# Another order of positions in theta/phi's first product, and a ScalarE copy moved ahead of the last plain half

## The chip, the cores and the metric

One core of one Trainium2 chip runs the whole program. The metric is the device time of one execution in microseconds, the median over several runs.

## The reference

Two layers work on eight images of 512 channels by 1024 positions (32 by 32), all in fp32. Cut to what matters:

```python
# layer 0: attention over positions, 8 heads of 64 channels
q, k, v = (conv1x1(x, W, b) for W, b in ((Wq, bq), (Wk, bk), (Wv, bv)))   # 512 -> 512
attn = softmax(einsum('bhdn,bhdm->bhnm', q, k) / 8)
x = x + conv1x1(einsum('bhnm,bhdm->bhdn', attn, v), Wp, bp)
# layer 1: non-local block, 256 inner channels
g, theta, phi = (conv1x1(x, w, b) for w, b in (g, theta, phi))            # 512 -> 256
f = einsum('bcn,bdn->bcd', theta, phi) / n
z = conv1x1(einsum('bcd,bdn->bcn', f, g), W, Wb) + x
out = batchnorm(z)                     # mean and variance over all images and positions
```

## The kernel before

**Images and stages.** `unshifted` walks over the images in a loop `for b in range(B)`. For each image it runs attention, then the projections q, v and k of image b+1 (`heads_of`, `values`), then the output projection of image b (`project`, PSUM tiles `pp`), theta and phi (`theta_phi`, tiles `ptp`), g (`pg`), and the product with W (`pz`).

**Products by quarters.** A matrix product is split as Strassen's scheme with Winograd's sums does it: seven products of quarter matrices in place of eight, with sums and differences made on VectorE (DVE) and GpSimd (POOL). Some of the seven are nested, which means that the quarter product is again split into seven small ones.

- `six` makes q, v and k of images 1 to 7. Its function `plain` first makes the one product that isn't nested, in two halves of 128 output channels. Each half goes to a PSUM bank of its own and is read twice by ScalarE (ACT) through `begin`: once into a temporary, `T6` (in the profile `T_pq` or `T_pk`), and once into the quarter "11" of the result (`q` or `k`). Then `six` goes through three pairs of nested products in the hand-written order

```python
    ORDER = "0a 0b 1a 2a 2b 1b 5a 4a 5b 4b 3a 3b 6a 6b".split()
```

where the digit is the small product and the letter the member of the pair. Each small product is added into PSUM, on top of what its chain already holds, and what the chain holds is read out before the next product of that chain is put on top. Where the reading is the first one of a result quarter, it is a ScalarE copy (line 479); otherwise it is a VectorE add (line 481). In the first pair, member a goes to quarter "11" (adds) and member b to quarter "12" (copies). Small products 0, 2 and 4 of a member share one chain; 1 and 3 share another. The four PSUM tiles s0 to s3 are used in turn: the plain halves take two of them, the four slots of the first pair are taken after these, and so slot 2 (products 1a, 5a, 3a) reuses the tile of the first plain half and slot 3 (products 1b, 5b, 3b) that of the second.

- `project` ends, for images 1 to 6, with the nested product `(1, "21", "11")`: its small products are added by VectorE (line 504) onto quarter "11" of the image `x`, which is channel blocks 0 and 1 and positions 0 to 511. These adds come in pieces of one channel block and 256 positions. In the order of the small products (`SEVEN`) the last four pieces are: block 0 positions 256 to 511, block 1 positions 256 to 511, block 0 positions 0 to 255, block 1 positions 0 to 255.

- `theta_phi` calls `seven` with `inner="tp"` for images 1 to 7. Its first product, "11", multiplies quarter "11" of `x` by a weight quarter. Positions are the rows of the result, so `x` is the operand that is loaded as weights: four parts i of 128 positions, and for each part two matmuls, one for each channel block k (line 391).

**What sets the order.** The framework's planner orders the instructions of each engine by its own cost model, except where the kernel pins one behind everything traced ahead of it on its engine (`pe`, `dve`, `sp`). All matmuls are pinned, and most VectorE sums here. The ScalarE reads of the plain halves and the copies are not pinned. The engines wait for one another by semaphores, and a matmul's wait sits on its weight load.

**How a matmul shows.** Each fp32 matmul of the program appears as two records of TensorE (PE), each with a weight load (PEld) of its own.

Of the kernel before, what the change touches and what calls it, by code (L numbers as in the profile page):

```python
# [10 lines left out]
AF = mybir.ActivationFunctionType  # L11
# [5 lines left out]
P = 128  # L17
# [13 lines left out]
def unshifted(ctx: ExitStack, tc: tile.TileContext, a: dict, out: bass.AP):  # L31
    nc = tc.nc
# [320 lines left out]
    def seven(name, w, data, positions_out, first, add, between=None, early=False,  # L353
              by_chunk=False, inner=None, via=()):

        nk, half = w.shape[2], w.shape[3]
        tags = list(free)
        free[:] = [tags[3], tags[1], tags[0], tags[2]] if early else [tags[3], tags[1], tags[2], tags[0]]  # L360
        slots, begun = {}, set()
        steps, counts = iter(()), iter(())
        if inner:
            free[:] = [tags[0], tags[2], tags[1], tags[3]] if inner == "p" else [tags[1], tags[2], tags[3], tags[0]]
            products, goes_to, counts = INNER[inner]
            counts = iter(counts)
            steps = nested(name, w, data, tags[2:], first, add, goes_to, positions_out)
        else:
            products = LATER if early == "later" else EARLY if early else SEVEN

        def read(reads, ps):
            for to, is_first in reads:
                (first if is_first else add)(to, ps)

        for n, (what, wi, di, s, reads) in enumerate(products):
            if s not in slots or early and what == "t4" or inner == "p" and what == "s3t3":
                slots[s] = bank(tags[s], f"{name}_{s}_{n}")
                begun -= {one for one in begun if one[0] == s}
            ps, d = slots[s], data[di]
            if positions_out:  # L380
                parts = [(ps.rearrange("p h (i f) -> p (h i) f", f=half)[:, i, :], i * half // 512,
                          lambda k, i=i: d[:, k, i * P:(i + 1) * P], lambda k: w[:, wi, k, :])
                         for i in range(512 // P)]
            else:
                parts = [(ps[:, m, :], m, lambda k, m=m: w[:, wi, k, m * P:(m + 1) * P], lambda k: d[:, k, :])
                         for m in range(half // P)]
            work = [(*part, k) for part in parts for k in range(nk)]
            if by_chunk and what in ("11", "s1t1"):
                work.sort(key=lambda one: one[4])
            for i, (to_ps, at, lhsT, rhs, k) in enumerate(work):  # L390
                pe(nc.tensor.matmul(to_ps, lhsT(k), rhs(k), start=(s, at) not in begun, stop=(k == nk - 1),  # L391
                                    skip_group_check=True))
                begun.add((s, at))
                for _ in range(next(counts, 0)):
                    next(steps)
            if inner and what in via:
                via[what](reads, ps)
            else:
                read(reads, ps)
            if between and n in between:  # L400
                between[n]()
# [4 lines left out]
    def six(name, w, data, positions_out, at, begin, third, fills, by_scalar=False, later=None):  # L406

        fills = dict(fills)
        shape = [P, 4, 256] if positions_out else [P, 2, 512]
        temps = {}  # L410

        def to(q):
            if q[0] != "T":
                return at(q)
            if q not in temps:
                temps[q] = w3.tile(shape, F32, tag="acc", name=f"{q}_{name}")
            return temps[q]

        def piece(q, i, j):
            if positions_out:  # L420
                return to(q)[:, j * 2:j * 2 + 2, i * P:(i + 1) * P]
            return to(q)[:, i, j * 256:(j + 1) * 256]

        def add(q, of, engine=None):
            dve((engine or nc.gpsimd).tensor_tensor(to(q), to(q), to(of), ALU.add))

        def plain():
            d = data["11"]
            for half in range(2):
                ps = next_bank(f"{name}_0_{half}")[:, 0, :]  # L430
                if positions_out:
                    ps = ps.rearrange("p (i f) -> p i f", f=256)
                for i in range(2 if positions_out else 1):
                    for k in range(2):
                        if positions_out:
                            at = (half * 2 + i) * P
                            pe(nc.tensor.matmul(ps[:, i, :], d[:, k, at:at + P], w[:, 0, k, :],  # L437
                                                start=(k == 0 and i == 0), stop=(k == 1), skip_group_check=True))
                        else:
                            pe(nc.tensor.matmul(ps, w[:, 0, k, half * P:(half + 1) * P], d[:, k, :],  # L440
                                                start=(k == 0), stop=(k == 1), skip_group_check=True))
                for q in ("T6", "11"):
                    at_ = to(q)[:, half * 2:half * 2 + 2, :] if positions_out else to(q)[:, half, :]
                    begin(at_, ps, half)
            load_w("first")

        plain()
        for one in fills.pop("plain", ()):
            one()
        for n, pair in enumerate(SIX):  # L450
            if n == 2:
                add("12", "22")
                add("12", "T6")
                for one in fills.pop("middle", ()):
                    one()
            slots = [next_bank(f"{name}_in_{n}_{i}") for i in range(4)]
            free[:] = [free[2], free[3], free[0], free[1]]
            begun = set()
            for step, which in enumerate(ORDER):
                _, wi, di, chain, reads = SEVEN[int(which[0])]  # L460
                m = "ab".index(which[1])
                outer, of, q = pair[m]
                a, d = w.inner(outer)[wi], data[f"inner {of}"][di]
                ps = slots[m if not chain else 2 + m][:, chain // 2, :256]
                start = (m, chain) not in begun
                begun.add((m, chain))
                if positions_out:
                    ps = ps.rearrange("p (i f) -> p i f", f=P)
                    for i in range(2):
                        pe(nc.tensor.matmul(ps[:, i, :], d[:, i * P:(i + 1) * P], a, start=start and not i, stop=True,  # L470
                                            skip_group_check=True))
                else:
                    pe(nc.tensor.matmul(ps, a, d, start=start, stop=True, skip_group_check=True))  # L473
                for (i, j), is_first in reads:
                    i, j = int(i) - 1, int(j) - 1
                    if is_first and q == "T7":
                        third(piece(q, i, j), ps, piece("T6", i, j), i)
                    elif is_first and q not in ("11", "T6"):
                        nc.scalar.copy(piece(q, i, j), ps)  # L479
                    else:  # L480
                        dve(nc.vector.tensor_tensor(piece(q, i, j), piece(q, i, j), ps, ALU.add))  # L481
                for one in fills.pop((n, step), ()):
                    one()
            load_w()
        assert not fills, fills
        if by_scalar:
            add("T7", "T6")
        ends = [lambda q=q: add(q, "T7") for q in ("22", "21")]
        if later is not None:
            later += ends  # L490
            return
        for one in ends:
            one()
# [68 lines left out]
    def heads_of(b, what, w, bias, data, pin=lambda ins: None, steps=None, fills=None, **how):  # L562
# [2 lines left out]

        if fills is not None:
            def begin(to, ps, i):
                nc.scalar.activation(to, ps, AF.Identity, bias=bias[:, i:i + 1])

            def third(to, ps, of, i):  # L570
                if what == "q":
                    nc.scalar.activation(to, ps, AF.Identity, bias=steps[:, i:i + 1])
                else:
                    dve(nc.vector.scalar_tensor_tensor(to, ps, steps[:, i:i + 1], of, ALU.add, ALU.add))

            six(f"p{what}_{b}", w, data, False, lambda q: t[:, rows(q), cols(q)], begin, third, fills,
                what == "q", how.get("later"))
            return t
# [919 lines left out]
```

## Time and profile before

| | |
|---|---|
| median of three runs | 2102.07 us (2102.05 to 2102.19) |
| profiled execution, its own time | 2102.2 us |
| its span, first to last instruction | 2100.4 us |
| TensorE busy | 2076.9 us (99%) |
| VectorE busy | 1442.6 us (69%) |
| ScalarE busy | 803.0 us (38%) |
| GpSimd busy | 818.3 us (39%) |
| mean granted TensorE clock | 0.996 |

The span is 1.8 us shorter than the execution's own time; the rest lies ahead of the first instruction and after the last. Busy TensorE time is a sum of records that overlap (a matmul's record ends after the next one has started), so a short wait can lie inside it.

### The profile page before, as it was taken

Reading aid. Unit: us, or ns where it says so; the run is one execution under the profiler, and the core shown is the slowest. Engines: PE = TensorE matmul, PEld = TensorE weight load, DVE = VectorE, ACT = ScalarE, POOL = GpSimd, SP = SyncE. Lnnn points to the kernel's source line nnn. Section 1 sums busy time; section 2 is a strip of 40 time slices with the busy share of each in tenths; the row PEclk is TensorE's granted clock in tenths of the full one; section 3 lists DMA queues with packets and bytes.
Section 4 is the critical chain, followed back from the end, with each engine's and each line's share of the span. In section 5 each row is a group of like instructions: output and inputs, shape, how many; then the busy total and the mean of one; then the engine's idle time right before and its main releaser. Section 6 shows DMA issues by size and latency. Waiting matters only on the chain.

```text
span 2100.4 us, 34471 instructions
## 1 busy us (share of the span) xinstructions
PE 2076.9 (99%) x13682; PEld 1176.0 (56%) x13682; DVE 1442.6 (69%) x2192; ACT 803.0 (38%) x1071; POOL 818.3 (39%) x689
## 2 busy tenths in 40 slices
PE   9999999999999999999999999999999999999995
PEld 4535864358733677336773377633876348743472
DVE  5587668775678656876567765677665775676756
ACT  1465204652046420564205641066312653056106
POOL 0024900448413583134922358223681338711010
PEclk9999999999999999999999999999999999999998
DMA  6254634445343443435324363153644345322668
GB/s 230 83 145 78 184 116 153 46 89 154 106 116 39 100 141 103 119 40 116 133 90 123 40 146 121 69 126 40 157 142 164 38 47 180 99 31 39 218 253 322
DMA packets 79697, 248.71 MB, mean 118 GB/s; under 512 B 17316, under 2 KB 25768, under 8 KB 77480
## 3 DMA queue, kind: packets, MB, share of 16 engines
q1 hardware_dynamic: 65656, 220.07, 32.3%
q0 software_dynamic: 12016, 24.80, 12.2%
q8 instruction: 110, 1.80, 0.4%
q10 hardware_dynamic: 1856, 1.56, 0.3%
q14 instruction: 59, 0.48, 0.1%
HBM read 164.64 MB, written 48.17 MB: 101 GB/s over the span
## 4 chain that ended last, share of the span: by engine, by line
PE 98%; ACT 1%; DVE 1%; DMA 0%; issue 0%
PE ps L638 21%; PE po L664 21%; PE ptp L391 7%; PE pv_in L470 6%; PE pp L391 6%; PE pk_in L473 6%; PE pq_in L473 6%; PE pg L391 5%; PE pz L391 3%; PE pp_in_s L342 3%; PE pf L916 2%; PE ptp_in_s L339 2%; PE pwf L959 1%; PE pv L437 1%; PE pq L440 1%; PE pq L391 1%
## 5 line engine op out<-in xcount | busy, mean ns | idle before, releaser
L641 ACT ACTIVATE e<-ps 128x1024 f32<-128x1024 f32 x512 | 523.0, 1025 | 412.0 <-PE ps L638 400.5
L694 POOL DMA_DIRECT2D fold<-acc x336 | 257.1, 816 | 921.7 <-DMA fold<-acc 543.3
L647 DVE TENSOR_TENSOR acc<-acc,e 128x1024 f32<-128x1024 f32 x384 | 469.9, 1224 | 93.2 <-ACT e L641 82.2
L638 PE MATMUL ps<-q,k 64*64 64x512 f32 x4096 | 529.2, 589 | 0.0
L664 PE MATMUL po<-e,v 64*64 64x512 f32 x4096 | 528.7, 589 | 0.0
L664 PEld LDWEIGHTS po<-e,v 64*64 64x64 f32 x4096 | 156.6, 133 | 282.9 <-issue 275.4
L638 PEld LDWEIGHTS ps<-q,k 64*64 64x64 f32 x4096 | 155.5, 133 | 283.2 <-issue 275.3
L947 ACT ACTIVATE g<-pg,gb 128x512 f32<-128x512 f32 x31 | 21.3, 688 | 366.5 <-PE pg L391 366.4
L645 DVE TENSOR_TENSOR acc<-e,e 128x1024 f32<-128x1024 f32 x64 | 78.3, 1224 | 114.5 <-ACT e L641 112.2
L391 PE MATMUL pp<-t_o,w_WpT 128*128 128x512 f32 x208 | 102.0, 592 | 0.0
L391 PE MATMUL ptp<-w_tp,t_x 128*128 128x256 f32 x400 | 96.1, 379 | 0.0
L756 POOL TENSOR_TENSOR o<-o,r 128x1024 f32<-128x1024 f32 x28 | 65.5, 2361 | 31.8 <-DMA r<-den_d 31.5
L391 PEld LDWEIGHTS ptp<-w_tp,t_x 128*128 128x128 f32 x400 | 72.3, 190 | 7.8
L821 POOL TENSOR_TENSOR x<-x,read 128x1024 f32<-128x1024 f32 x30 | 69.8, 2353 | 13.0 <-ACT read L818 13.0
L481 DVE TENSOR_TENSOR k<-k,pk_in 128x256 f32<-128x256 f32 x112 | 46.8, 421 | 39.5 <-PE pk_in L473 35.0
L391 PE MATMUL ptp<-w_tp,x 128*128 128x256 f32 x272 | 70.0, 381 | 0.8
L479 ACT COPY v<-pv_in 128x256 f32<-128x256 f32 x84 | 31.4, 374 | 95.0 <-DVE T_pv L481 25.5
L479 ACT COPY k<-pk_in 128x256 f32<-128x256 f32 x84 | 31.3, 372 | 92.0 <-PE pk_in L473 90.3
L481 DVE TENSOR_TENSOR v<-v,pv_in 128x256 f32<-128x256 f32 x112 | 46.3, 421 | 29.3 <-PE pv_in L470 22.8
L470 PE MATMUL pv_in<-w_WvT,i_t_x 128*128 128x128 f32 x448 | 59.2, 275 | 0.0
L473 PE MATMUL pk_in<-i_t_x,w_WkT 128*128 128x256 f32 x224 | 58.1, 381 | 0.1
L473 PE MATMUL pq_in<-i_t_x,w_WqT 128*128 128x256 f32 x224 | 57.5, 379 | 0.0
(250 smaller groups left out, 3249.6 us busy)
## 6 DMA issues: line engine op xcount, KB each, us to landing
fold<-acc POOLq DMA_DIRECT2D x336, 64.0 KB, 3.0
w_WqT<-kept_WqT SPq DMA_DIRECT2D x21, 896.0 KB, 5.8
w_WvT<-kept_WvT SPq DMA_DIRECT2D x21, 896.0 KB, 5.4
w_WkT<-kept_WkT SPq DMA_DIRECT2D x21, 896.0 KB, 6.6
r<-den_d SPq DMA_DIRECT2D x32, 512.0 KB, 6.8
x<-in_x_dram SPq DMA_DIRECT2D x30, 512.0 KB, 5.8
spill<-x SPq DMA_DIRECT2D x24, 512.0 KB, 4.0
z<-spill SPq DMA_DIRECT2D x24, 512.0 KB, 8.4
```

Source lines behind the costliest of these rows:

```text
L391: pe(nc.tensor.matmul(to_ps, lhsT(k), rhs(k), start=(s, at) not in begun, stop=(k == nk - 1), skip_group_check=True))
L470: pe(nc.tensor.matmul(ps[:, i, :], d[:, i * P:(i + 1) * P], a, start=start and not i, stop=True, skip_group_check=True))
L473: pe(nc.tensor.matmul(ps, a, d, start=start, stop=True, skip_group_check=True))
L481: dve(nc.vector.tensor_tensor(piece(q, i, j), piece(q, i, j), ps, ALU.add))
L638: pe(nc.tensor.matmul(ps[c * P // 2:(c + 1) * P // 2, j, :], k[r, p, keys], q[r, p, h * 512:(h + 1) * 512], start=True, stop=True, skip_gr ...
L641: nc.scalar.activation(e, ps, AF.Exp, scale=SCALE)
L645: nc.vector.tensor_tensor(accs[u], es[u, 0], e, ALU.add)
L647: ins = nc.vector.tensor_tensor(accs[u], accs[u], e, ALU.add)
L664: pe(nc.tensor.matmul(ps[j * D:(j + 1) * D, r, :], v[keys, m, (2 * p + j) * D:(2 * p + j + 1) * D], e[keys, j, :], start=(m == 0), stop=(m ...
L694: nc.gpsimd.dma_start(to, of, accum_op=ALU.add)
L756: dve((engine or nc.vector).tensor_tensor(at, at, of, ALU.mult))
L821: dve(nc.gpsimd.tensor_tensor(at, at, t, ALU.add))
```

## The change

There are two independent parts. In `theta_phi`'s first product, the four parts of 128 positions are taken in the order 2, 3, 0, 1 in place of 0, 1, 2, 3. In `six`, for q and k only, the second reading of the second plain half (the one into quarter "11") is held back: the ScalarE copy of the first nested product of member b (product 0b) is issued ahead of it, and both are pinned in that order. The number of instructions stays the same.

```diff
-                         for i in range(512 // P)]
+                         for i in ((2, 3, 0, 1) if inner and what == "11" else range(512 // P))]
...
         fills = dict(fills)
+        held_back = []
...
                 for q in ("T6", "11"):
                     at_ = to(q)[:, half * 2:half * 2 + 2, :] if positions_out else to(q)[:, half, :]
-                    begin(at_, ps, half)
+                    one = lambda at_=at_, ps=ps, half=half: dve(begin(at_, ps, half))
+                    if half and q == "11" and not positions_out:
+                        held_back.append(one)
+                    else:
+                        begin(at_, ps, half)
...
                     elif is_first and q not in ("11", "T6"):
-                        nc.scalar.copy(piece(q, i, j), ps)
+                        ins = nc.scalar.copy(piece(q, i, j), ps)
+                        if held_back:
+                            dve(ins)
                     else:
                         dve(nc.vector.tensor_tensor(piece(q, i, j), piece(q, i, j), ps, ALU.add))
+                if step == 1 and held_back:
+                    held_back.pop()()
...
             def begin(to, ps, i):
-                nc.scalar.activation(to, ps, AF.Identity, bias=bias[:, i:i + 1])
+                return nc.scalar.activation(to, ps, AF.Identity, bias=bias[:, i:i + 1])
```

## The prediction

> **What bounds the kernel now.** I read the page first, for the engine that sets the time.
>
> ```profile
> span 2100.4 us, 34471 instructions
> ...
> PE 2076.9 (99%) x13682; PEld 1176.0 (56%) x13682; DVE 1442.6 (69%) x2192; ACT 803.0 (38%) x1071; POOL 818.3 (39%) x689
> ...
> PE 98%; ACT 1%; DVE 1%; DMA 0%; issue 0%
> ```
>
> TensorE is the chain from start to end. A change that removes no matmul can win only the short waits between matmuls. The 99% hides some: a record of 256 fp32 columns lasts 379 ns (median), while back-to-back records start 216 ns apart, so a wait under 163 ns leaves no idle time. I therefore took the start of every matmul record, subtracted the pace of its kind, and looked for excess. The waits of the weight loads say who ended it:
>
> ```profile
> PEld ptp L391 <- issue: 4.0, 10, 0.5
> ...
> PEld pq_in L473 <- ACT q L479: 2.1, 7, 0.3
> PEld pk_in L473 <- ACT k L479: 2.1, 7, 0.3
> ```
>
> Columns: total us, times, longest. The copies of line 479 end a wait once in each of seven q and seven k stages. The theta/phi row is said to wait for nothing visible, but the timeline of one such place (image 2) shows what ends there:
>
> ```profile
> 791.32 0.85 DVE L504 TENSOR_TENSOR x<-x,pp_in_s 128x256 f32<-128x256 f32 x2 [0.87 <-PE pp_in_s L342]
> ...
> 792.84 0.59 PE L342 MATMUL pp_in_s<-i_o,w_WpT 128*128 128x256 f32 x2
> 793.04 0.85 DVE L504 TENSOR_TENSOR x<-x,pp_in_s 128x256 f32<-128x256 f32 x2 [0.87 <-PE pp_in_s L342]
> 793.53 0.60 PEld L391 LDWEIGHTS ptp<-w_tp,x 128*128 128x128 f32 x3 [0.50 <-issue]
> 793.56 0.67 PE L391 MATMUL ptp<-w_tp,x 128*128 128x256 f32 x2
> ```
>
> The last projection records start at 792.84 and 793.06, so theta/phi's first record was due at 793.27. Its weight load, part 0 of block 0, needs the add that starts at 793.04 and ends at 793.46; it starts 70 ns after that. The record starts 0.295 us late and the second loses 0.078 more: **0.373 us**, in images 1 to 6 alike (0.372 to 0.374). Image 7, whose projection isn't nested, shows none.
>
> The other place, in k of image 5:
>
> ```profile
> 1266.86 0.69 ACT L568 ACTIVATE T_pk<-pk,bk 128x512 f32<-128x512 f32 x1 [0.39 <-PE pk L440]
> ...
> 1267.45 0.68 ACT L568 ACTIVATE k<-pk,bk 128x512 f32<-128x512 f32 x1
> 1267.52 2.05 PE L473 MATMUL pk_in<-i_x,w_WkT 128*128 128x256 f32 x8
> 1268.02 0.37 ACT L479 COPY k<-pk_in 128x256 f32<-128x256 f32 x1
> 1268.23 0.78 DVE L481 TENSOR_TENSOR k<-k,pk_in 128x256 f32<-128x256 f32 x2 [0.44 <-ACT k L568]
> 1268.44 0.73 PEld L473 LDWEIGHTS pk_in<-i_x,w_WkT 128*128 128x128 f32 x4 [0.29 <-ACT k L479]
> 1269.18 0.37 ACT L479 COPY k<-pk_in 128x256 f32<-128x256 f32 x1 [0.79 <-PE pk_in L473]
> ```
>
> Product 2b adds onto 0b, so its load waits for 0b's copy. That copy starts at 1268.02, behind the second plain half, though 0b was complete at 1267.69. The load, due at 1268.17, starts at 1268.44. Record 2b loses 58 ns and the next 107: **0.165 us**, fourteen times.
>
> **What the skill says.** The Trainium skill, "Trainium Kernel Development and Optimization", Performance Expectations, calls matmul busy time a bad measure because matmuls are pipelined; the 0.165 us above with hardly any idle time on TensorE agree. "TensorE: Matmul & The Clock Gate", section "Wait — 56ns, not 53.3ns?", gives 215.7 ns start to start for 512 warm columns; here a record of 256 fp32 columns shows the same 216 ns. "PSUM — Partial Sum Buffer", section on bank collisions, says that two engines may not touch one bank at once and the hardware doesn't arbitrate. Its section "Engine vs sequencer instructions" calls ScalarE's and VectorE's queues strictly first-in first-out. The trace agrees: the load of 1a, which reuses the first plain half's bank, carries a ScalarE wait. These two matter for the held read.
>
> **Part 1, position order.** Nothing is added or removed. Parts 2 and 3 need the pieces of positions 256 to 511, whose adds end at 791.74 and 792.17, 1.1 us before 793.27. So the first four matmuls (eight records, 1.73 us) wait for nothing, and part 0 comes at 795.00, 1.1 us after its second piece (793.89). The stall goes: −0.373 us. That the planner tells positions apart within a channel block is seen in the projection, where GpSimd's add onto another quarter of the same blocks (positions 512 on) overlaps these VectorE adds. What is late next? Product s1t1 needs the difference `t_x`, which VectorE ends at 796.35 whatever TensorE does; its load was at 796.88 and moves to 796.51, 0.16 us of slack left. Product s2t2 adds onto "11", read by VectorE until about 799.87; its load comes at about 799.96. Tight, but a load may be some 0.11 us late before a matmul loses anything. GpSimd's inner differences are over 1 us ahead. So 6 × 0.373 = **2.24 us**. Ends: 0 (another wait on the same load) and 2.24; a loss is excluded, since parts 2 and 3 are ready earlier than 0 and 1.
>
> **Part 2, the copy ahead.** No DMA is moved and neither SP's nor POOL's queue is passed; on ScalarE one copy and one activation change places.
> - The copy can start 38 ns after 0b's end (as the copy of 2b does, 1269.14 to 1269.18): 1267.724. It ends at 1268.095, and the load 50 ns later at 1268.145, ahead of 1268.17. **Stall at 2b gone: −0.165.**
> - The held activation follows. Copy and then activation aren't seen side by side at this size. The one such pair (128x256 copy, one-column activation) starts 0.27 us apart, and without overlap it would be 0.37. I take 0.27, as the back-to-back 128x512 pairs here overlap by about 0.1 too: start 1267.99, end 1268.67 (0.68 us), against 1268.13 before.
> - **It adds a wait on TensorE.** Slot 3 reuses the second plain half's tile, so 1b must wait for the held read; before, the wait for the later copy covered it. Load at 1268.67 + 0.05 = 1268.72. A load that is late lets its record run 0.105 us on (1268.441 to 1268.546 above): 1268.829, due 1268.819. Loss 0.01.
> - **It adds a wait on VectorE.** The add of 1a writes the held half. It starts 32 ns after the activation (that step is 32 ns all through attention), at 1268.71 in place of 1268.23; behind it stands the add of 2a, then nothing until 5a is done. Product 5a's load waits for the add of 1a (its VectorE wait lies between those for 0a and 2a): 1268.71 + 0.42 + 0.05 = 1269.18, record 1269.287, due 1269.262. Loss 0.03. Product 4a waits for the add of 2a: end 1269.49, record possible 1269.65, due 1269.71. No loss. In q a 0.42 us difference stands between these adds and fits in.
>
> So 0.165 − 0.04 = 0.125 us, × 14 = **1.75 us**; ends 0 and 2.31 (no residual). A later start of the held read by 0.1 us costs 0.1 at both 5a and 1b together, which is the lower end.
>
> **Sum.** 2.24 + 1.75 = 3.99 us: profiled execution 2102.2 to 2098.2, span 2100.4 to 2096.4; the median of the runs stands 0.1 below that execution, so 2102.07 − 3.99 = **2098.1 us** (−0.19%). Later stages follow TensorE, so nothing hands the gain back; one k stage (image 3, at 765.6) has an irregular wait of 0.41 us for VectorE, which may swing by a few tenths.
>
> **Rivals.** A change of 0.2%, 4.2 us, is about what a measurement of this kernel can tell from no change.
> 1. *Both parts, more complete:* the residual is nil, and the 0.05 us stall at the end of five k stages shifts too: 2102.07 − 2.24 − 2.31 − 0.25 = 2097.3. For it: the residual is only two margins of some 10 and 30 ns. Against: both wake-ups are measured.
> 2. *The wait only changes place:* the held read ends 0.1 us or more later than worked out, and 1b and 5a lose what 2b wins: 2102.07 − 2.24 = 2099.8. For it: the chain from the held read over the add to 5a has no slack at all.
> 3. *Part 1 does nothing,* because the first load waits for something else that comes at the same time (weights, a released bank): 2102.07 − 1.75 = 2100.3. Against: the load follows the add's end in all six images.
> 4. *Slower:* the held read is pinned, and the planner's order puts it behind one more ScalarE instruction, the copy of 2b. That copy starts at 1269.02 (2b ends 1268.98), the held read 0.27 later at 1269.29 and ends at 1269.97, and record 1b runs at 1270.12 in place of 1268.82. That is 1.3 us × 14 = 18.2 us, less the 4.55 of both stalls: 2115.7. It decides from (4.2 + 4.55) / 14 = 0.63 us a place on. Against: the program traces the held read right after the first copy, and a pin orders it behind nothing later.
>
> **How the numbers follow.** The worked-out case 64%, rival 1 9%, rival 2 16%, rival 3 6%, rival 4 and its like 5%. The worked-out case spans 2097.5 to 2098.9, and 2097.87 (−0.2%) lies inside it, below the centre: four tenths of it, 26%, are faster by over 0.2%, and with rival 1 that is 35%. Within 0.2%: 60%. Slower: 5%. The range 2097.0 to 2100.2 holds the first three.
>
> **What would show it.** Right: in the waits of the weight loads, the two rows of the line 479 copies vanish, and line 391's "issue" row falls by about six waits of 0.5 us; the longest matmul of `ptp<-w_tp,x` falls from 455 ns to 379. In its place the loads of `pk_in` and `pq_in` wait for the held read and the add of 1a, 0.15 to 0.2 us each, and the add of 1a idles about 0.9 us in place of 0.44. Wrong: a new excess of over 0.1 us at 1b or 5a, or at s1t1, or a median outside 2097.0 to 2100.2.

## The result, and the profile after

The changed kernel takes 2098.82 us (median of 22 runs, 2098.2 to 2099.32), and the kernel before, in the same set of runs, 2102.43 us. The ratio is 0.9982, with a 95% interval of 0.9976 to 0.9988: 3.6 us or 0.17% less. The prediction had the likeliest time at 2098.1 us, 0.7 us lower, and a gain just under 0.2%. The page of the kernel after, in the lines that the prediction shows of before:

```profile
span 2097.2 us, 34471 instructions
...
PE 2074.6 (99%) x13682; PEld 1175.8 (56%) x13682; DVE 1444.2 (69%) x2192; ACT 804.1 (38%) x1071; POOL 818.1 (39%) x689
...
PE 98%; ACT 1%; DVE 1%; DMA 0%; issue 0%
```

The same instructions on the same engines, a span 3.2 us shorter, and TensorE still the chain. The shares can't show what happened. The waits of the weight loads do (total us, times, longest):

```profile
PEld pq_in L478 <- ACT q L577: 1.1, 7, 0.2
PEld pq_in L478 <- DVE q L488: 1.1, 7, 0.2
PEld pk_in L478 <- DVE k L488: 1.1, 7, 0.2
PEld pk_in L478 <- ACT k L577: 1.1, 7, 0.2
...
PEld ptp L391 <- issue: 1.0, 4, 0.2
```

The rows of the copies (line 479 before, 484 now) are gone. Two new waits stand in their place, in seven q and seven k stages: for the held read (line 577) and for VectorE's add (line 488). In each, the weight-load unit idles 1.1 / 7 = 0.16 us; most of that costs TensorE nothing, as shown below. The "issue" row of theta/phi fell from ten waits and 4.0 us to four and 1.0: six waits of 0.5 us are gone. The timeline of the changed kernel in image 2, where theta/phi begins:

```profile
792.45 0.59 PE L342 MATMUL pp_in_s<-i_o,w_WpT 128*128 128x256 f32 x2
792.65 0.85 DVE L513 TENSOR_TENSOR x<-x,pp_in_s 128x256 f32<-128x256 f32 x2 [0.87 <-PE pp_in_s L342]
792.66 3.43 PEld L391 LDWEIGHTS ptp<-w_tp,x 128*128 128x128 f32 x16
792.88 3.62 PE L391 MATMUL ptp<-w_tp,x 128*128 128x256 f32 x16
...
794.74 1.21 DVE L282 TENSOR_TENSOR t_x<-x 128x1024 f32<-128x1024 f32 x1
...
796.12 0.84 PEld L391 LDWEIGHTS ptp<-w_tp,t_x 128*128 128x128 f32 x4
```

The last projection records start at 792.45 and 792.66, and the first theta/phi record 0.216 us later, at full pace, while VectorE is still at its last two adds. The next possible wait, for `t_x`, was close: `t_x` is ready at 795.95 and the load that needs it starts at 796.12. The k stage of image 5:

```profile
1265.40 0.69 ACT L577 ACTIVATE T_pk<-pk,bk 128x512 f32<-128x512 f32 x1 [0.39 <-PE pk L441]
...
1266.07 1.91 PE L478 MATMUL pk_in<-i_x,w_WkT 128*128 128x256 f32 x8
1266.27 0.37 ACT L484 COPY k<-pk_in 128x256 f32<-128x256 f32 x1 [0.18 <-PE pk_in L478]
1266.53 0.69 ACT L577 ACTIVATE k<-pk,bk 128x512 f32<-128x512 f32 x1
1267.26 0.75 DVE L488 TENSOR_TENSOR k<-k,pk_in 128x256 f32<-128x256 f32 x2 [0.93 <-ACT k L577]
1267.28 0.30 PEld L478 LDWEIGHTS pk_in<-i_x,w_WkT 128*128 128x128 f32 x2 [0.16 <-ACT k L577]
...
1267.73 0.30 PEld L478 LDWEIGHTS pk_in<-x,w_WkT 128*128 128x128 f32 x2 [0.16 <-DVE k L488]
```

The copy now waits for TensorE alone, and the held read follows it. Three things then hang on the end of that read: the load of 1b (1267.28), VectorE's add of 1a (1267.26), and through that add the load of 5a (1267.73). Each of the two loads is 0.13 us behind its place. Some 0.107 us of that costs nothing, and the records lose 0.024 us each: the one after the late load starts 239 ns after its forerunner in place of 216.

### The profile page after: what moved, and what is told of

It reads as the page before. It is cut to its first block, busy times and chain, and to the rows that moved or that the text cites. A ratio compares the mean times of both kernels' runs of the same rounds, so it can differ in the third digit from the quotient of the medians.

```text
span 2097.2 us, 34471 instructions
## 1 busy us (share of the span) xinstructions
PE 2074.6 (99%) x13682; PEld 1175.8 (56%) x13682; DVE 1444.2 (69%) x2192; ACT 804.1 (38%) x1071; POOL 818.1 (39%) x689
## 4 chain that ended last, share of the span: by engine, by line
PE 98%; ACT 1%; DVE 1%; DMA 0%; issue 0%
PE ps L647 21%; PE po L673 21%; PE ptp L391 7%; PE pv_in L475 6%; PE pp L391 6%; PE pk_in L478 6%; PE pq_in L478 6%; PE pg L391 5%; PE pz L391 3%; PE pp_in_s L342 3%; PE pf L925 2%; PE ptp_in_s L339 2%; PE pwf L968 1%; PE pv L438 1%; PE pq L441 1%; PE pq L391 1%
```

## The experiments

The theory: two separate sets of short TensorE waits became shorter, and nothing else changed. The rivals: the gain comes from elsewhere (another order by the planner, the start-up), or the waits only change place. The measure for both is the excess: the start of each matmul record less the start of the one before it, less the pace of its kind. The pace is the usual distance of two starts in these traces: 216 ns for 256 columns, 429 for 512, 112 for 128. The prediction names 216 ns too, but its 0.295, 0.078 and 0.165 us come out of the recorded starts only with about 213 ns, and the expectations below carry these figures on. With 216 the same starts give 0.367 us a place in theta/phi and 0.159 us a place in q and k. Summed over the places in question (us; excesses of over 10 ns; the start-up is the first 12 us):

| kernel | theta/phi's first records, 6 places | first pair of q and k, 14 places | start-up | median, us |
|---|---|---|---|---|
| before | 2.20 | 2.23 | 2.10 | 2102.43 |
| changed | 0 | 0.65 | 2.75 | 2098.82 |
| part1_only | 0 | 2.24 | 2.63 | 2100.39 |
| part2_only | 2.20 | 0.68 | 3.13 | 2101.38 |
| after_again | 0 | 0.67 | 2.57 | 2098.94 |
| order_2013 | 0 | 0.66 | 2.20 | 2098.51 |
| order_0231 | 2.20 | 0.66 | 2.24 | 2100.83 |
| t6_held | 0 | 0.34 | 2.71 | 2098.50 |
| t6_held_again | 0 | 0.34 | 2.17 | 2098.78 |
| t6_split | 0 | 0 | 2.55 | 2098.10 |
| t6_late | 0 | 18.47 | 2.73 | 2116.64 |

These columns account for the spans. The span of each trace less its three sums is 2093.8 to 2093.9 us in eight of the eleven. The other three (part2_only, t6_held, t6_split) have one more wait of 0.23 to 0.30 us in the projection of image 0, at about 262 us, and t6_held one of 0.26 us at 16 us; with these taken off, they agree too. t6_held_again, the same kernel as t6_held, has neither, so such waits vary between executions of one kernel; what ends them is open.

The two orders were run once, the others in several rounds. The kernel before had a median of 2102.6 beside the first four experiments (part1_only, part2_only, after_again, t6_held), 2102.72 beside the two orders and t6_late, and 2102.66 beside t6_split and t6_held_again.

### Each part alone, and both again

part1_only is the kernel before with this one edit; part2_only is the changed kernel with it undone; after_again is the changed kernel once more.

```diff
-                         for i in range(512 // P)]
+                         for i in ((2, 3, 0, 1) if inner and what == "11" else range(512 // P))]
```

> Only the order 2, 3, 0, 1 of positions in theta/phi's first product; ScalarE as before. Theory (two separate sets of short TensorE waits): the late first record of theta/phi is gone in images 1 to 6 (6 x 0.373 = 2.24 us), and the 0.165 us at product 2b of q and k stays fourteen times; time against before -2.2 us (about -0.11%), the excess of record starts over their pace down by 2.24 us. Rival (the gain of the whole change comes from elsewhere, the planner's other order or the start-up): less than 1 us, or the excess vanishes and comes back at product s1t1.

> Only the ScalarE copy ahead of the held read; positions in the old order. Theory: 2b loses nothing, 1b and 5a lose 0.026 us each as in the changed kernel, so 14 x (0.165 - 0.052) = 1.58 us less; time against before -1.6 us (about -0.08%); theta/phi's first record stays 0.29 us late in six images. Rival (the wait only changes place): no gain.

> The changed kernel once more, beside its two halves on one chip. Theory: the sum of the halves, 2.24 + 1.58 = 3.8 us less than before; the start-up, where the first records run at half pace for a varying while, moves single runs by some tenths. Rival (the halves overlap or help one another): the whole differs from the sum by over 1 us.

Measured against before's 2102.6: part1_only −2.2 us (ratio 0.999, 0.9983 to 0.9996), part2_only −1.2 us (0.9993, 0.9985 to 1.0001, so by time alone it isn't told from no change), both −3.7 us (0.9982, 0.9975 to 0.9989). By the clock the halves sum to 3.4 us, 0.2 less than the whole, which is within the intervals. The waits of the weight loads separate them cleanly. Of part1_only:

```profile
PEld pk_in L473 <- ACT k L479: 2.1, 7, 0.3
PEld pq_in L473 <- ACT q L479: 2.1, 7, 0.3
...
PEld ptp L391 <- issue: 1.0, 4, 0.2
```

And of part2_only:

```profile
PEld ptp L391 <- issue: 4.0, 10, 0.5
...
PEld pk_in L478 <- ACT k L577: 1.1, 7, 0.2
...
PEld pk_in L478 <- DVE k L488: 1.1, 7, 0.2
```

Each part removes its own row of waits and leaves the other's as it was before. In the table the two columns add up: 2.20 for the first part, 2.23 − 0.68 = 1.55 for the second, 3.75 together. The excess nowhere comes back, since the rest of the span is the same in all kernels. So the gain does not come from elsewhere; what the start-up adds is said further below.

### Which part has to come first

order_2013 and order_0231 are the changed kernel with another order of positions.

```diff
-                         for i in ((2, 3, 0, 1) if inner and what == "11" else range(512 // P))]
+                         for i in ((2, 0, 1, 3) if inner and what == "11" else range(512 // P))]
```

> The changed kernel with the positions of theta/phi's first product in the order 2, 0, 1, 3: one part of cover (two matmuls, 0.86 us) in place of two. Theory (each weight load waits for the pieces of its own positions alone): part 0 is loaded at about 0.65 us after its place in the old order, 0.4 us after its piece is there, so no late record in the six images, as with 2, 3, 0, 1. Rival (the planner makes the load wait for the whole channel block, or for two parts' worth of time): 0.1 to 0.37 us late, six times.

```diff
-                         for i in ((2, 3, 0, 1) if inner and what == "11" else range(512 // P))]
+                         for i in ((0, 2, 3, 1) if inner and what == "11" else range(512 // P))]
```

> The changed kernel with the order 0, 2, 3, 1: only which part comes first is as before. Theory: the first load waits for the late piece again, 0.295 + 0.078 = 0.373 us in six images, 2.2 us in all. Rival (the gain comes from part 1 being taken late, or from the PSUM half that is written first): the wait is smaller or gone.

The matmul row of theta/phi, with the least, median and longest duration of a record in ns. That of order_2013:

```profile
L391 PE MATMUL ptp<-w_tp,x x272: 379/379/382, 278.0 to 2008.5; 128*128 128x256 f32 x136
```

And that of order_0231:

```profile
L391 PE MATMUL ptp<-w_tp,x x272: 379/379/455, 278.1 to 2010.7; 128*128 128x256 f32 x136
```

In order_0231 the longest record is 455 ns again, as before the change, with the same 2.20 us of excess. So only the part that comes first counts. In order_2013 part 0 is loaded 0.86 us after theta/phi's first load (792.12 and 792.98 in image 2; the expectation has 0.65) and 0.46 us after its own piece is there, so one part of cover is enough, and a load waits for the pieces of its own positions. One run each (2098.51 and 2100.83 us, 2.3 us apart) agrees with the 2.20 us between them.

### Which read is held back

t6_held holds back the read into T6 in place of the one into quarter "11"; t6_held_again is the same kernel on another occasion.

```diff
-                    if half and q == "11" and not positions_out:
+                    if half and q == "T6" and not positions_out:
```

> The whole change, but the read of the second plain half that is held back is the one into the temporary T6, not the one into quarter 11. VectorE's add of 1a then finds its half written early, and only TensorE's 1b waits for the held read. Theory: the 0.026 us at 5a goes, the 0.026 us at 1b stays; 14 x 0.026 = 0.36 us less than the changed kernel, about 4.2 us less than before. Rival (5a waits for something else, or the loss moves on to 4a): no difference from the changed kernel in the record starts.

> t6_held once more, beside t6_split on one chip. Theory: about 4.1 us less than before and 0.37 us more than t6_split, which is near what one set of runs can tell; the record starts decide.

The excess of the first pairs halves, from 0.65 us to 0.34 in both, all of it at 1b: 0.024 us a place. In the waits of t6_held's weight loads the rows for VectorE's add are gone, and only those for the held read are left:

```profile
PEld pk_in L478 <- ACT T_pk L577: 1.1, 7, 0.2
PEld pq_in L478 <- ACT T_pq L577: 1.1, 7, 0.2
```

So the loss at 5a came through VectorE's add of 1a alone. The times, 2098.50 and 2098.78, lie 0.04 to 0.44 us under those of the changed kernel (2098.82 and 2098.94), so that the gain of 0.31 us over the changed kernel is read from the records and not from the clock.

### How much a late read costs

t6_late is t6_held with the held read issued only behind the copy of 2b. Against the changed kernel its edit is that of t6_held and this one:

```diff
-                if step == 1 and held_back:
+                if step == 4 and held_back:
```

> As t6_held, but the held read is issued only behind the copy of product 2b (step 4 in place of step 1). This makes the price of a late held read large. Theory (1b, which reuses the bank, waits for the held read): the held read ends at about 1269.98 in the old clock of image 5, record 1b starts 1.3 us late, fourteen times: 18 us more than t6_held, about 2116.7 us. Rival (1b waits for VectorE or for the copy of 0b, as it seemed before the change): under 2 us more.

2116.64 us, ratio 1.0066 (1.005 to 1.0083), and 18.47 us of excess, 18.47 / 14 = 1.32 us a place. Its timeline in the k stage of image 5:

```profile
1278.97 0.37 ACT L484 COPY k<-pk_in 128x256 f32<-128x256 f32 x1 [0.92 <-PE pk_in L478]
1279.24 0.69 ACT L577 ACTIVATE T_pk<-pk,bk 128x512 f32<-128x512 f32 x1
1279.99 0.30 PEld L478 LDWEIGHTS pk_in<-i_x,w_WkT 128*128 128x128 f32 x2 [1.46 <-ACT T_pk L577]
1279.99 0.70 PE L478 MATMUL pk_in<-i_x,w_WkT 128*128 128x256 f32 x2 [1.05 <-ACT T_pk L577]
```

The load of 1b starts when the held read ends, and TensorE has nothing else: the wait is now long enough to show as idle time. This is the wait that the prediction's slower rival describes. It shows that the wait at 1b is for the held read, a wait that the profile before could not show, since the later wait for the copy of 0b covered it.

### A read in two pieces

t6_split starts from t6_held. There ScalarE could start another instruction 0.586 us after it starts the read into "11" (the distance of two such reads back to back), and the copy of 0b starts 0.28 us later than that. Reading half of the columns of T6 nearly fits in between.

```diff
-                    one = lambda at_=at_, ps=ps, half=half: dve(begin(at_, ps, half))
                     if half and q == "T6" and not positions_out:
-                        held_back.append(one)
+                        begin(at_[:, :256], ps[:, :256], half)
+                        held_back.append(lambda at_=at_[:, 256:], ps=ps[:, 256:]: dve(begin(at_, ps, 1)))
```

> As t6_held, but the second half's read into T6 is split by columns: 256 of them are read ahead of the copy of product 0b, in the 0.28 us in which ScalarE only waits for 0b, and 256 behind it. Theory: the copy starts about 0.1 us later, still early enough for 2b (its load may be 0.1 us late); the rest of the read ends about 0.1 us earlier than in t6_held, so that 1b loses nothing any more. 14 x 0.026 = 0.37 us less than t6_held, about 4.5 us less than before; no excess of record starts left in the first pairs. Rival (the fixed cost of one more ScalarE read pushes the copy too far): 2b loses again, 0.05 us or more at each of 14 places.

2098.10 us, ratio 0.9978 (0.997 to 0.9986), 4.6 us less than before. Its k stage of image 5:

```profile
1265.07 0.47 ACT L577 ACTIVATE T_pk<-pk,bk 128x256 f32<-128x256 f32 x1 [0.39 <-PE pk L441]
...
1265.45 0.68 ACT L577 ACTIVATE k<-pk,bk 128x512 f32<-128x512 f32 x1
...
1265.74 1.89 PE L478 MATMUL pk_in<-i_x,w_WkT 128*128 128x256 f32 x8
1266.02 0.38 ACT L484 COPY k<-pk_in 128x256 f32<-128x256 f32 x1
1266.27 0.50 ACT L577 ACTIVATE T_pk<-pk,bk 128x256 f32<-128x256 f32 x1
```

ScalarE runs through without a gap. The copy of 0b starts some 0.08 us later than it could, which costs nothing, and no excess of over 4 ns is left in the first pair at any of the 14 places. So this version is ahead of both kernels in the records: 0.65 us less than the changed kernel and 0.34 less than t6_held. By time it is 0.72 us below the changed kernel, though on different occasions, and 0.68 us below t6_held_again beside it. That is more than the records give, and a time difference of this size is not told from chance by these runs.

## Why the prediction was right, point by point

- **The bound.** TensorE, short waits alone: right. Of the waits between matmuls, only those at the listed places changed with the edits. What else differs between traces is the start-up and the single waits named above.
- **The size of the stalls.** The prediction subtracts a pace of about 213 ns and not the 216 ns that it names, so 0.373 and 0.165 us are too large by 3 ns a record: 0.367 and 0.159. Its own due times for 1b show it: 1268.98 in the trace less 1268.82 is 0.16. With 216 ns its terms give 6 × 0.367 = 2.20 us for part 1 and 14 × (0.159 − 0.04) = 1.67 us for part 2, 3.87 us in all.
- **Part 1.** Measured 2.20 us in the records and 2.2 by time. The slack at s1t1, 0.16 us by the prediction, was 0.17 (795.95 to 796.12). That the planner tells positions apart is now shown by the order of parts alone.
- **Part 2, the copy.** It started 37 ns after 0b's end (38 worked out), and the wait at 2b is gone in all 14 places.
- **Part 2, the residual, 0.04 us a place.** Measured 0.047. 1b lost 24 ns where 10 were worked out, and 5a 24 where about 25 were. The start of the held read behind the copy was as taken (0.268 us after it, 0.27 assumed), so the pair that the trace before had only at another size was a fair price. The activation itself took 0.692 us in place of 0.680, and the load that waits for it started 52 ns after its end in place of 50; these are the 14 ns. The chain behind it, ScalarE to VectorE to 5a, held to a few ns, and 4a lost nothing, as said. So part 2 brought 1.55 to 1.58 us in place of 1.75.
- **The sum.** Predicted 3.99 us; the records say 3.75 to 3.78, the clock 3.6 and 3.7. The median lies 0.7 us above the likeliest time for two reasons of about equal size: the gain was 0.38 us smaller than forecast, and the kernel before has a median of 2102.43 us over 22 runs, 0.36 above the three runs from which the forecast starts.
- **What it didn't consider.** The single profile of before was a short one in the start-up: 2.10 us of excess there, against 2.17 to 3.13 in the other ten profiles. Some of the first full-size records start more than one pace apart, and how many do so differs from run to run. Of the 3.78 us, 0.65 (2.75 − 2.10) is given back there in the profiled pair, which makes the spans 3.2 us apart. Whether this also accounts for the 0.1 to 0.2 us between records and medians can't be said, since only one run of each set has a trace.
- **Range and rivals.** The median lies within 2097.0 to 2100.2. Rival 2, the wait that only changes place, happened to under a third: 0.65 of 2.23 us. Rival 4's mechanism is real and its price was right (1.3 us a place predicted, 1.32 measured in t6_late), but the change doesn't trigger it. Rival 1's vanished residual is what t6_split reaches; the 0.05 us stalls at the end of k stages are still there. The four tenths that the prediction puts on the fast side of 2097.87 us don't follow from its own span: 2097.5 to 2098.9 us, evenly spread, has about a quarter there.

## What to carry to other kernels

On an engine that is 99% busy, look for short waits in the starts of its records, not in its idle time, and price each against the pace; a few hundredths repeated 14 times can be forecast if every wake-up, and the pace itself, is taken from the same trace. Then check that the span less the named waits is the same in all versions: here this leaves no room for another cause. Before a read of a PSUM bank is moved back, list everything that reuses that bank and everything queued behind the reader's consumer: a wait that another one covers isn't in the profile, and moving the cover away uncovers it. Where the operands of a step become ready piece by piece, let the step begin with the piece that was ready first; one part of cover was enough here.

## What the runs showed of the hardware that was not expected

The pace at the start of the program differs between executions of the same work. In the first 4.4 to 4.6 us the records of the small warm-up product start 213 ns apart, nearly twice the 112 ns of a 128-column fp32 record later on, and the first full-size records are up to 0.85 us apart in place of 0.43: none by that much in the profile of before, two in that of the changed kernel. Other profiles lose up to 0.85 us instead at about 9 us (t6_held), where a load waits for the DMA of a weight. Over all profiles the start moved by up to 1.0 us (2.10 to 3.13), more than a quarter of the whole effect. The Trainium skill's page "TensorE: Matmul & The Clock Gate", section "What's actually happening", says that the point at which the clock rises varies from run to run, by ±500 ns. These traces agree in kind, but spread wider: the slow distance ends at 4.4 us in order_2013, and two records up to 6.35 us still have it in the changed kernel.

A 128x512 activation behind a copy took 0.692 us and not the 0.680 of the same activation behind another activation. It is small, but it was most of what the forecast of part 2 lacked at 1b.
